# A decoder layer on one core: when an attention output projection is drawn as filler, and which queue fetches the last rows

## The chip, the cores and the metric

The kernel runs on one core of one Trainium2 chip. Its engines work in parallel, each through its own instructions in order: TensorE (PE in the profile, its weight loads PEld), VectorE (DVE), ScalarE (ACT), GpSimd (POOL) and SyncE (SP), which here only issues DMAs. DMAs issued by SP and ACT go through hardware queues, those issued by GpSimd through a software queue (q0 in the profile). The metric is the device time of one launch in microseconds, as the median of three runs, and it is to be small.

## The reference

Eight batches of 256 tokens with 512 features pass through one decoder layer in float32, with a plain layer norm (no weights) after each of three sublayers:

```
x = norm(x + attention(x))              # 16 heads of 32; Wq, Wk, Wv, then Wdown per head; softmax; Wup; Wo
r[t] = decay * r[t-1] + ctx[t]**2       # a running sum over the tokens of a batch, per feature
x = norm(x + x * r)                     # the "cross attention"
x = norm(x + silu(x @ gate.T) * (x @ up.T) @ down.T)   # 2048 wide; weights interpolated from control points
```

Wdown and Wup are folded into the projection weights by the kernel, so that a head is projected once.

## The kernel before, in words

The 2048 tokens are handled in four groups of 512 (`NG`), each of two batches. Attention runs as 32 steps, `steps[s] = (g, bb, quad)`: a step does four heads (`quad`) of one batch (`n = 2 * g + bb`). Steps 0 to 7 are the first group, 16 to 23 the third, 24 to 31 the last. I number them from 0, as the code does; batches too, so that the fifth batch is n = 4.

A step (lines 751 to 824) does this, each engine in the order of the program (`Ordered`, line 299):

- TensorE makes the scores of the *next* step (`scores(s + 1)`) in four PSUM buffers of the pool `ps_big`, then transposes the exponentials of this step, `es[0]` to `es[2]`, into buffers of `ps_mm` (tile `tr_e`). VectorE takes the maxima of the next scores (`nmax`), ScalarE their exponentials (`e`); the transposes are copied out (`eT`), the first and third by VectorE, the second and fourth by ScalarE.
- `fill(2)` draws two yields of filler, then the fourth transpose follows, then `fill(6)` (in the last group `fill(2)`).
- In odd steps the reciprocals of the softmax sums are spread and transposed (`tr_rec`, copied to `yT`). Then `weighted` multiplies the probabilities with the values into `av`. One `av` buffer serves two steps; it is read by VectorE (`yT = av * yT`) after the third transpose of the step after the odd one.

The pool `ps_mm` has four buffers. `tr_e`, `tr_rec`, `av`, the projections (`ps_q`, `ps_k`, `ps_v`), the output projection (`ps_o`), the transposes of the running sum (`tr_r`), and those of the feed-forward inputs (`tr_x`, `ps_mom`) all take their buffers from it.

Filler is a list of `units`, generators of which each `next` issues a piece for TensorE. A unit of four yields is one 128-row block of a projection of the next group (`project`, line 467, one matmul a yield, the eviction with the last), or one half of a batch's output projection (`output`, line 570). In the last group there are, in place of projections, `inputs(0)` and `inputs(1)` (line 700), eight yields each: four of transposes with their copies (`x2T`) and the DMAs to `xd`, and four of moment matmuls with copies (`mom`) and the DMAs to `md`. Before the scores of a new group, all units other than outputs are drawn to the end, in `fill(4)`.

Beside the units there are `chains`: `recur(n)` (line 485), which fetches the squared-to-be context `r` of a batch, squares it on GpSimd and runs four scans on VectorE, and `norms(n, qc, ...)` (line 589), which finishes 128 tokens after their output projection: the first norm (`nm`, a Square on ScalarE, `va` and `rs` on GpSimd, `x1`), the transposes of `r` (`tr_r`), then `h2`, `mx`, and the second norm. Every odd pass of a `fill` gives each chain one turn (`slot()`), and draws 0.62 of a weight chunk (`some_taps`). `recur` has its DMA in the first turn, the square in the third and the scans in the fifth to eighth; `norms` issues `tr_r` in its fourth turn and reads it in its fifth.

The tokens' rows for the residual come by `load_rows` (line 562) into the pool `rows`, of six buffers. At the first step of each batch n, the rows and the output projection of batch n - 1 are put up, and `recur(n)` is started. After step 31 the feed-forward part begins: `gate_up` (tiles `pg`, `pu`) for the first 512 tokens, then `fill(8)` with the output projection of batch 7, then the matmuls `y`.

Of the kernel before, what the change touches and what calls it, by code (L numbers as in the profile page):

```python
# [17 lines left out]
P = 128  # L18
B, T, D = 8, 256, 512
# [7 lines left out]
NG = NT // GT  # L27
# [288 lines left out]
def decoder_kernel(ctx: ExitStack, tc: tile.TileContext, x, xT, ctxT, wq, wkT, wvT, woT, wdownT, wup, decay, up_taps, down_taps, mom_f, sum_f, out, plan):  # L316
    nc = tc.nc
# [27 lines left out]
    nc = Ordered(tc)  # L345
    units, chains = [], []

    def slot():

        for c in list(chains):  # L350
            if next(c, c) is c:
                chains.remove(c)

    def fill(n):

        for i in range(n):
            if units:
                next(units[0][1])
                units[0][2] -= 1
                if not units[0][2]:  # L360
                    units.pop(0)
            if i % 2:
                slot()
                some_taps()
# [76 lines left out]
    def some_taps():  # L441
        made[0] += 0.62
        while made[0] >= 1:
            made[0] -= 1
            next(weights, None)
# [39 lines left out]
    def recur(n):  # L485

        r = last.tile([P, DC, T], F32, tag="r", name="r", bufs=2)
        nc.sync.dma_start(out=r, in_=ctxT[:, n * T : (n + 1) * T].rearrange("(c p) t -> p c t", p=P))
        rs[n] = r
        yield  # L490
        yield
        nc.gpsimd.tensor_tensor(r, r, r, ALU.mult)
        yield
        yield
        for ch in range(DC):
            nc.vector.tensor_tensor_scan(
                r[:, ch, :], dec[:, ch : ch + 1].to_broadcast([P, T]), r[:, ch, :], 0.0, ALU.mult, ALU.add
            )
            yield
# [61 lines left out]

    def load_rows(n):
        xs[n] = []
        for qc in range(2):
            x_t = rows.tile([P, D], F32, tag="row", name="x_t")
            r0 = (n * 2 + qc) * P
            nc.sync.dma_start(out=x_t, in_=x[r0 : r0 + P, :])
            xs[n].append(x_t)

    def output(n, qc):  # L570
# [112 lines left out]
    def windows(xd, xt, xg):  # L683


        past = SPAN * ND - D
        nc.sync.dma_start(out=xd[4 * (SPAN - past) + 3 :: 4, :], in_=xt[:past, 0, :])
        for h, odd, n, j0 in ((0, 0, NTILE // 2 - 1, 1), (1, NTILE - 1, NTILE // 2 - 1, 0)):
            for t, m, j in ((odd, 1, odd // 2), (2 * j0 + h, n, j0)):
                step = 4 * (lows[t + 2][0] - lows[t][0]) if m > 1 else 0  # L690
                from_ = bass.AP(xd.tensor, xd.offset + 4 * lows[t][0] * GT, [[GT, RAW], [step * GT, m], [1, GT]])
                nc.sync.dma_start(out=xg[h * K2 : h * K2 + RAW, j : j + m, :], in_=from_)
# [7 lines left out]
    def inputs(b):  # L700

        pool, mf = ffn["pool"], ffn["mf"]
        xt = pool.tile([P, DC, GT], F32, tag="x2T", name="x2T")
        xd = ffn["dram"].tile([4 * SPAN, GT], F32, tag="xd", name="xd")
        md = ffn["dram"].tile([1, 20 * NTILE, GT], F32, tag="md", name="md")
        xg = pool.tile([P, NTILE // 2, GT], F32, tag="xg", name="xg", bufs=2)
        xgs[b] = xg
        for c in range(DC):
            tr = ps_mm.tile([P, GT], F32, tag="mm", name="tr_x2")
            for t in range(TC):  # L710
                nc.tensor.transpose(tr[:, t * P : (t + 1) * P], x2[:, b * TC + t, c * P : (c + 1) * P], ident)
            (nc.vector.tensor_copy if c % 2 else nc.scalar.copy)(xt[:, c, :], tr)
            nc.gpsimd.dma_start(out=xd[c : 4 * (P - 1 - c) + c + 1 : 4, :], in_=xt[c:, c, :])
            if c:
                row = 4 * (SPAN - c) + c - 1
                nc.sync.dma_start(out=xd[row : row + 4 * c - 3 : 4, :], in_=xt[:c, c, :])
            yield
        if b > 1:
            reads.append(lambda: windows(xd, xt, xg))
        else:  # L720
            windows(xd, xt, xg)
        mo = ffn["mom"].tile([P, ND, GT], F32, tag="fin", name="mom")
        ps = {}
        for c in range(DC):
            for s in (c, c + 1):
                if s // 2 not in ps:
                    ps[s // 2] = ps_mm.tile([P, GT], F32, tag="mm", name="ps_mom")
                at = slice(s % 2 * K2, (s % 2 + 1) * K2)
                nc.tensor.matmul(
                    ps[s // 2][at, :],  # L730
                    lhsT=mf[:, c, s - c, :],
                    rhs=xt[:, c, :],
                    start=(s == c + 1 or c == 0),
                    stop=(s == c or c == DC - 1),
                )
            if c == 1:
                nc.vector.tensor_copy(mo[:, 0, :], ps[0])
            if c == DC - 1:
                nc.vector.tensor_copy(mo[:, 1, :], ps[1])
                nc.scalar.copy(mo[:K2, 2, :], ps[2][:K2, :])  # L740
                nc.gpsimd.dma_start(out=md[:, : 2 * P].rearrange("h (c p) t -> (h p) c t", p=P), in_=mo[:, :2, :])
                nc.gpsimd.dma_start(out=md[0, 2 * P :], in_=mo[:K2, 2, :])
                if b > 1:
                    reads.append(lambda: moments(md, xg))
                else:
                    moments(md, xg)
            yield
# [4 lines left out]
    for s, (g, bb, quad) in enumerate(steps):  # L752
        n = g * 2 + bb
        if quad == 0 and bb == 0:
            if g + 1 < NG:
                units += projections(g + 1, xT_g)
            else:
                first.close()
                open_inputs()
                units += [["i", inputs(0), 2 * DC], ["i", inputs(1), 2 * DC]]  # L760
        if quad == 0 and n:
            load_rows(n - 1)
            o = [["o", output(n - 1, qc), DC] for qc in range(2)]
            if bb and g + 1 < NG:
                units[1:1] = o[:1]
                units.append(o[1])
            else:
                units[1:1] = o
            chains.append(recur(n))
        more = s + 1 < len(steps)  # L770
        if more and steps[s + 1][0] != g:
            while any(u[0] != "o" for u in units):
                fill(4)
            if g + 2 < NG:
                xT_g = load_x(g + 2)
        if more:
            sc = scores(s + 1)
        after = []

        def ahead(j):  # L780
            if more:
                after.append(exponentials(s + 1, j, sc[j]))

        if quad % 2:
            rec = small.tile([P, 2, 8], F32, tag="rec", name="rec")
            nc.vector.reciprocal(rec, sums[n][:, :, quad // 2 * 8 : quad // 2 * 8 + 8])
            wide = att.tile([P, 2, 8, DH], F32, tag="wide", name="wide")
            nc.vector.tensor_copy(wide, rec.unsqueeze(3).to_broadcast([P, 2, 8, DH]))
        tr0 = transposed(es[0])
        ahead(0)  # L790
        eTs = [evicted(tr0, nc.vector.tensor_copy)]
        tr1 = transposed(es[1])
        tr2 = transposed(es[2])
        if pending is not None:
            y, av = pending
            nc.vector.tensor_tensor(y, av, y, ALU.mult)
            pending = None
        eTs.append(evicted(tr1, nc.scalar.copy))
        ahead(1)
        eTs.append(evicted(tr2, nc.vector.tensor_copy))  # L800
        fill(2)
        tr3 = transposed(es[3])
        ahead(2)
        eTs.append(evicted(tr3, nc.scalar.copy))
        ahead(3)
        fill(6 if g + 1 < NG else 2)
        if quad % 2:
            tr = ps_mm.tile([P, 2, T], F32, tag="mm", name="tr_rec")
            for q in range(2):
                for qc in range(2):  # L810
                    nc.tensor.transpose(
                        tr[:, q, qc * P : (qc + 1) * P],
                        wide[:, qc, q * 4 : q * 4 + 4, :].rearrange("p h r -> p (h r)"),
                        ident,
                    )
            y = last.tile([P, 2, T], F32, tag="yT", name="yT", bufs=4)
            nc.scalar.copy(y, tr)
            yTs.setdefault(n, []).append(y)
        else:
            av = ps_mm.tile([P, 2, T], F32, tag="mm", name="av")  # L820
        weighted(s, eTs, av)
        if quad % 2:
            pending = y, av
        es = after
# [202 lines left out]
```

## Time and profile before

| | us |
|---|---|
| median of three runs | 604.07 (603.5 to 604.6) |
| the profiled execution | 603.72 |
| its span, first to last instruction | 601.9 |
| TensorE busy | 577.3 (96%) |
| VectorE busy | 335.5 (56%) |
| ScalarE busy | 277.9 (46%) |
| GpSimd busy | 219.3 (36%) |

How to read it. The page gives busy time by engine, then the chain of work that ended last: from the last instruction back, at each step to what released it, or to the instruction before it on its engine. A line of a group reads "engine line operation out<-in, shape, count", then busy time and mean; in the timeline a line begins with its start and length in us, and ends in brackets with the idle time of the engine before it and what ended that. All instructions come from one helper (line 308), so tiles tell them apart. A matmul's end is modelled, so that a wait within a run of matmuls shows as a longer run. A 128x512 float32 matmul of the program stands as two MATMUL records in the trace.

### The profile page before, as it was taken

How to read it: one execution, taken by the hardware profiler on the slowest of the kernel's cores; microseconds unless marked ns; L12 is line 12 of the kernel's file. 1: busy time of each engine (PE TensorE's matmuls, PEld its weight loads, DVE VectorE, ACT ScalarE, POOL GpSimd, SP SyncE). 2: the span in 40 equal slices, each digit the busy share in tenths (PEclk: the TensorE clock that was granted, in tenths of full speed). 3: DMA queues.
4: the chain of work that ended last, by engine and by line, in shares of the span. 5: the costliest groups of instructions: out<-in, count | busy, mean ns of one | idle time of the engine just before them, and what ended most of it. 6: DMA issues, size and time to landing. Idle time of an engine off the chain costs nothing.

```text
span 601.9 us, 9688 instructions
## 1 busy us (share of the span) xinstructions
PE 577.3 (96%) x3346; PEld 292.0 (49%) x3346; DVE 335.5 (56%) x742; ACT 277.9 (46%) x820; POOL 219.3 (36%) x495
## 2 busy tenths in 40 slices
PE   9999999998899999999999999999999999999993
PEld 4544555555455555554554555444444434433432
DVE  0203634658676665886674777776926605714614
ACT  0114643655654554655455667665315404504502
POOL 0000997065544336444340311300272262142244
PEclk9999999999999999999999999999999999999998
DMA  8104253034224115323210564659328986984931
GB/s 294 64 0 157 80 167 114 27 98 144 74 71 141 36 54 175 105 71 96 79 36 2 158 152 102 173 152 216 65 72 223 205 233 179 227 213 134 212 142 70
DMA packets 38961, 75.50 MB, mean 125 GB/s; under 512 B 3937, under 2 KB 8289, under 8 KB 38913
## 3 DMA queue, kind: packets, MB, share of 16 engines
q1 hardware_dynamic: 34576, 62.75, 39.4%
q0 software_dynamic: 3328, 10.96, 5.5%
q10 hardware_dynamic: 1008, 1.18, 0.7%
q8 instruction: 26, 0.43, 0.3%
q14 instruction: 23, 0.18, 0.1%
HBM read 42.86 MB, written 11.04 MB: 90 GB/s over the span
## 4 chain that ended last, share of the span: by engine, by line
PE 82%; DVE 10%; ACT 3%; DMA 2%; issue 2%; POOL 1%; POOLq 0%; DVEq 0%; SPq 0%; ACTq 0%
PE y L308 12%; PE ps_k L308 9%; PE ps_v L308 9%; PE ps_o L308 8%; PE ps_q L308 6%; PE tr_e L308 6%; PE sc L308 5%; PE pg L308 5%; PE ps_s L308 5%; PE av L308 5%; PE pu L308 5%; DVE nmax L308 3%; PE ps_mom L308 2%; ACT e L308 2%; DVE eT L308 2%
## 5 line engine op out<-in xcount | busy, mean ns | idle before, releaser
L308 ACT ACTIVATE e<-sc,nmax 128x256 f32<-128x256 f32 x256 | 120.2, 480 | 102.1 <-DVE nmax L308 102.1
L308 DVE TENSOR_REDUCE nmax<-sc 128x2 f32<-128x512 f32 x128 | 84.5, 682 | 73.6 <-PE sc L308 67.7
L308 POOL TENSOR_TENSOR taps<-taps 128x256 f32<-128x256 f32 (+1 forms) x144 | 89.0, 618 | 33.1 <-DMA taps<-in_down_taps 26.3
L308 PEld LDWEIGHTS tr_e<-ident,e 128*128 128x128 f32 x512 | 56.9, 140 | 25.2 <-issue 22.5
L308 PE MATMUL tr_e<-ident,e 128*128 128x128 f32 x512 | 68.3, 276 | 0.5 <-DVE eT L308 0.4
L308 PE MATMUL y<-inter,wd 32*128 32x512 f32 x512 | 63.0, 598 | 0.0
L308 PE MATMUL ps_o<-w_o,yT 128*128 128x512 f32 x128 | 60.0, 600 | 2.6 <-DVE eT L308 2.3
L308 PE MATMUL ps_k<-xT_g,w_k 128*128 128x512 f32 x128 | 58.8, 601 | 0.6 <-DVE eT L308 0.6
L308 PE MATMUL ps_v<-w_v,xT_g 128*128 128x512 f32 x128 | 58.6, 598 | 0.4 <-DVE eT L308 0.4
L308 PE MATMUL ps_q<-xT_g,w_q 128*128 128x512 f32 x128 | 58.2, 596 | 0.0
L308 POOL TENSOR_SCALAR va<-ss 128x1 f32<-128x1 f32 x32 | 7.3, 227 | 136.8 <-ACT x L308 86.6
L308 POOL TENSOR_TENSOR rs<-va,neghalf 128x1 f32<-128x1 f32 x48 | 28.9, 602 | 69.4 <-DVE va L308 66.7
L308 ACT ACTIVATION_READ_ACCUMULATOR e<-sc,nmax 128x1 f32 x256 | 53.2, 208 | 0.0
L308 DVE TENSOR_TENSOR inter<-pu,sg 128x512 f32<-128x512 f32 x64 | 41.2, 686 | 18.3 <-PE pu L308 9.4
L308 ACT ACTIVATE sg<-pg 128x512 f32<-128x512 f32 x64 | 37.2, 596 | 18.4 <-PE pg L308 18.4
L308 DVE COPY eT<-tr_e 128x512 f32<-128x512 f32 x64 | 43.8, 684 | 0.5 <-PE tr_e L308 0.4
L308 PEld LDWEIGHTS y<-inter,wd 32*128 32x128 f32 x512 | 26.7, 184 | 32.7 <-issue 27.0
L308 PE MATMUL av<-eT,v_g 128*32 128x256 f32 x512 | 36.7, 385 | 5.0 <-ACT eT L308 2.7
L308 ACT COPY eT<-tr_e 128x512 f32<-128x512 f32 x64 | 37.5, 585 | 2.4 <-PE tr_e L308 2.4
L308 POOL TENSOR_TENSOR r<-r 128x1024 f32<-128x1024 f32 x8 | 15.2, 1895 | 63.6 <-DMA r<-in_ctxT 63.6
L308 PE MATMUL sc<-k_g,q_g 32*128 32x256 f32 x512 | 37.4, 401 | 0.2 <-ACT e L308 0.2
L308 PEld LDWEIGHTS ps_o<-w_o,yT 128*128 128x128 f32 x128 | 22.8, 190 | 26.4 <-issue 21.5
(98 smaller groups left out, 737.5 us busy)
## 6 DMA issues: line engine op xcount, KB each, us to landing
nat<-inter SPq DMA_DIRECT2D x64, 256.0 KB
taps<-in_down_taps SPq DMA_DIRECT2D x40, 256.0 KB
taps<-in_up_taps SPq DMA_DIRECT2D x16, 384.0 KB
xg<-xd SPq DMA_DIRECT2D x8, 616.0 KB
r<-in_ctxT SPq DMA_DIRECT2D x8, 512.0 KB
x_t<-in_x SPq DMA_DIRECT2D x16, 256.0 KB
fin<-sum POOLq DMA_DIRECT2D x16, 256.0 KB, 5.1
out<-h SPq DMA_DIRECT2D x16, 256.0 KB
```

The lines of the kernel that those rows point to most:

```text
L308: return lambda *a, **k: self.tc.keep_in_program_order(f(*a, **k))
```

## The change

- Projection and output yields drawn after the fourth transpose: 6 in the first two groups as before, 5 in the third, 3 in the last (2 before).
- In the third group, at its second batch, both halves of the output projection of batch 4 are put at the end of the units; before, the first half stood second and the other at the end.
- In the last group, at its first batch, the output projection of batch 5 is put ahead of the last unit, and the rows of batch 5 and `recur(6)` come two steps later (at quad 2). At its second batch the rows of batch 6 are put up with the output projection as before, and `recur(7)` comes two steps later.
- Rows of batches 5, 6 and 7, and the context of batches 6 and 7, are fetched by GpSimd's queue in place of SP's.

```diff
     def recur(n):
 
         r = last.tile([P, DC, T], F32, tag="r", name="r", bufs=2)
-        nc.sync.dma_start(out=r, in_=ctxT[:, n * T : (n + 1) * T].rearrange("(c p) t -> p c t", p=P))
+        (nc.sync if n + 2 < 2 * NG else nc.gpsimd).dma_start(out=r, in_=ctxT[:, n * T : (n + 1) * T].rearrange("(c p) t -> p c t", p=P))
...
     def load_rows(n):
         xs[n] = []
+        queue = nc.sync if n + 3 < 2 * NG else nc.gpsimd
         for qc in range(2):
             x_t = rows.tile([P, D], F32, tag="row", name="x_t")
             r0 = (n * 2 + qc) * P
-            nc.sync.dma_start(out=x_t, in_=x[r0 : r0 + P, :])
+            queue.dma_start(out=x_t, in_=x[r0 : r0 + P, :])
...
                 units += [["i", inputs(0), 2 * DC], ["i", inputs(1), 2 * DC]]
+        if n and quad == (0 if g + 1 < NG else 2):
+            if g + 1 < NG or not bb:
+                load_rows(n - 1)
+            chains.append(recur(n))
         if quad == 0 and n:
-            load_rows(n - 1)
             o = [["o", output(n - 1, qc), DC] for qc in range(2)]
-            if bb and g + 1 < NG:
+            if bb and g + 2 == NG:
+                units += o
+            elif bb and g + 2 < NG:
                 units[1:1] = o[:1]
                 units.append(o[1])
+            elif g + 1 == NG and not bb:
+                units[-1:-1] = o
             else:
+                if g + 1 == NG:
+                    load_rows(n - 1)
                 units[1:1] = o
-            chains.append(recur(n))
...
-        fill(6 if g + 1 < NG else 2)
+        fill((6, 6, 5, 3)[g])
```

## The prediction

> **What bounds the kernel now.** I read the page first: which engine is busy, and which ends the chain of waits.
>
> ```profile
> span 601.9 us, 9688 instructions
> PE 577.3 (96%) x3346; PEld 292.0 (49%) x3346; DVE 335.5 (56%) x742; ACT 277.9 (46%) x820; POOL 219.3 (36%) x495
> PE 82%; DVE 10%; ACT 3%; DMA 2%; issue 2%; POOL 1%; POOLq 0%; DVEq 0%; SPq 0%; ACTq 0%
> ```
>
> TensorE carries 82% of the chain. The change neither adds nor removes a matmul, so only TensorE's waits can move the time. The sums by window (span, length, then busy time of PE, PEld, DVE, ACT, POOL) show where they are: the third group of tokens (steps 16 to 23, and the end of step 15), the last group (24 to 31), the head of the feed-forward part.
>
> ```profile
> 230.88:323.60 92.72, 92.16 (x545) 49.80 (x545) 62.62 (x144) 51.74 (x172) 39.88 (x74) 1.00 0.28 88
> 331.62:402.40 70.78, 64.56 (x496) 37.09 (x493) 54.62 (x128) 45.98 (x154) 15.83 (x25) 1.00 0.56 146
> 402.40:424.28 21.88, 21.88 (x93) 9.85 (x89) 15.33 (x34) 12.78 (x24) 1.49 (x4) 1.00 0.98 214
> ```
>
> Only the last group has room: 6.2 us of visible idle time, and matmuls stretched by waits inside them. The waits of TensorE in that window name the causes: evictions (x2T, mom, eT) that come late.
>
> ```profile
> PE av L308 <- DVE x2T L308: 2.3, 2, 1.2
> PE av L308 <- ACT eT L308: 1.3, 2, 1.0
> PE tr_rec L308 <- DVE mom L308: 0.8, 1, 0.8
> PE ps_mom L308 <- DVE mom L308: 0.8, 1, 0.8
> ```
>
> The resource behind it is the pool ps_mm, four PSUM buffers for everything but scores. One is always av (kept from an even step until the yT multiply of the next even step). The three transposes that open a step take the others. Step 7 has no filler, so its fourth transpose asks for a fifth buffer and waits for the first eT, which DVE ended at 139.97. TensorE's order of time there:
>
> ```profile
> 138.10 1.53 PE L308 MATMUL tr_e<-ident,e 128*128 128x128 f32 x12
> 140.03 0.66 PE L308 MATMUL tr_e<-ident,e 128*128 128x128 f32 x4 [0.39 <-DVE eT L308]
> ```
>
> Step 29 shows what a fuller pool costs: with av, a moment sum and tr_r held, the fourth transpose waits for a moment copy, and the last moment matmul for the eviction after it.
>
> ```profile
> 374.66 1.15 PE L308 MATMUL sc<-k_g,q_g 32*128 32x256 f32 x16
> 375.74 1.53 PE L308 MATMUL tr_e<-ident,e 128*128 128x128 f32 x12
> 377.20 1.98 PE L308 MATMUL ps_mom<-x2T,mf 128*64 128x512 f32 x8
> 379.11 0.66 PE L308 MATMUL tr_r<-ident,r 128*128 128x128 f32 x4
> 379.92 0.66 PE L308 MATMUL tr_e<-ident,e 128*128 128x128 f32 x4 [0.15 <-DVE mx L308]
> 380.51 1.94 PE L308 MATMUL ps_mom<-x2T,mf 128*64 128x512 f32 x6
> 383.23 1.07 PE L308 MATMUL ps_mom<-x2T,mf 128*64 128x512 f32 x2 [0.78 <-DVE mom L308]
> ```
>
> **The change, part by part.** A unit of filler is four yields; one yield of projection is two 128x512 matmuls, 0.86 us. Before, a step draws 2 and then 6 (last group: 2), so every unit ends inside its step. After, the third group draws 2+5 and the last 2+3: units straddle steps and hold a buffer across the opening transposes.
>
> What is moved, by counting yields: the third group has 64 (48 of projections, 8 each of batches 3 and 4). Steps 16 to 22 serve 49; at step 23 the loop that empties projections serves 8 ahead of the scores, and 2+5 the remaining 7. So the matmuls of batch 4 (the fifth) still end in step 23; their norms go to the last group. There 32 yields are served 5 a step, so that step 30 gets 2 and step 31 none.
>
> Third group. The third transpose normally starts 0.97 us after the first (two of three in 1.46): 376.71 in step 29. With a unit held it waits for the first eT, as the moment matmul at 377.20 did: +0.49. With tr_r held too, the second waits to 377.20, ends at 377.69, ACT's eT takes to 378.4, and the third starts at 378.45: +1.74. Units are held into steps 17, 18, 21, 22 and 23. Into step 19 both are, since with three slots a step the fourth slot of norms (x1, tr_r) of batch 3's second half falls last in step 18, and h2, which frees the buffer, in the next. 5 x 0.49 + 1.74 = 4.2. Two waits of 0.44 at steps 17 and 19 lie at the same place; I take +3.8. TensorE is 92.16 of 92.72 busy, so nothing covers this and a gain over 0.6 is excluded. Bounds 0 (the buffer handed out happens to be free) to +4.6.
>
> Last group, step by step, each time from the start of its scores, by these rows: DVE pitch 0.6 (nmax, eT, copy, h1, h2, mx, scan), ACT 0.91 for a pair of e, 0.47 to 0.58 for a copy, 0.8 for a Square. Now 8.54, 9.34, 8.61, 8.02, 8.53, 11.16, 9.25, 7.33 (start to start of scores; the last ends at 402.40).
> Step 24: four transposes of x2 as now, plus one moment yield in the wait ahead of av: 8.8.
> Step 25: av, the moment buffer and tr_r are held. Transposes at 1.08, 2.54, 3.8; the second moment yield needs the buffer of the third eT, 5.15; two moment yields to 6.9, tr3 to 7.4, the fourth to 8.35. DVE meanwhile does copy, h2, mx ahead of the third nmax, so that e ends at 8.8, eT at 9.4 and the copy of the moment sums at 9.15; two output yields and tr_r run from there to 11.35, tr_rec waits for ACT's copy, 11.9, av 12.9.
> Step 26: a unit and tr_r held. The unit ends within the first fill (5.35), and DVE's h1, h2, mx stand ahead of nmax: nmax 8.2, e 9.2, eT 9.8, the last 5/8 of av 0.65: 10.5.
> Step 27: h1 and a norm ahead of nmax, tr_r and three tr_x share the free buffers; the third x2T comes from ACT at 9.0, then tr_rec and av: 10.6.
> Step 28: norm, scan, h2 and mx ahead of nmax: 8.9, e 9.9, eT 10.45; av ends at 12.0.
> Step 29: 8.77 of work and 1.74 for two held: 10.5.
> Step 30: two yields; h1, a norm and two Squares ahead: eT 8.45: 9.15.
> Step 31: 7.33 less four yields (3.43) plus 0.9 of bare eviction: 4.8.
> The sum is 79.25 for 70.78: +8.5. Lower bound: step 7 without filler took 7.92 (137.03 to 144.95); if steps 24 to 29 kept their lengths, with 8.88 where 5 yields fill one (+1.1), step 30 fell to 7.9 and step 31 to 4.9, it would be -2.6. Between these ends I take the upper: step 29's row shows the wait itself.
>
> GpSimd's queue. Six row loads (128 pieces of 2 KB) and two of r (512 pieces of 1 KB) move from SP to POOL. The nearest issue on POOL is xd, of 128 pieces:
>
> ```profile
> L308 POOL DMA_DIRECT2D xd<-x2T x16: 530/552/775, 337.2 to 502.2; - x16
> DMA to landing us min/median/max: 2.3/3.5/4.8
> ```
>
> 6 x 0.55; md with 256 pieces took 0.75 to 0.82, so I estimate 1.3 for r: 5.9 us of POOL, which is busy 15.8 of 70.8. What is queued behind is va and rs of the norms. SP loses eight issues of about 0.4, with nobody waiting: h never waited for x_t. I cost the loads at nothing; the cover is that x_t of batch 5, issued about when step 26 starts behind md, lands by 2 to 4 and h1 comes at 5.45. If it lands as late as md did at worst (9.3), h1 and all behind it on DVE come 3.5 us later: that is the upper end of the last group, +12.
> The Trainium skill ("DMA: Bandwidth & Descriptors", Specifications) speaks against this part: first byte after about 1 us by GpSimd, 0.6 by the sync path. If all eight loads were on the path, that would be 3.2 us more; by the rows none is.
>
> Moved later: scans of batch 7 (four of 0.68 on DVE) go into the head of the feed-forward part, where DVE is busy 15.3 of 21.9, hidden under matmuls. Moved earlier from there: two groups of tr_r, 0.44 each on TensorE: -0.9 (bounds -0.9 and 0). Taps: 92 slots are needed, reached in step 22 before and in step 23 after; the weights are read at 402, so nothing.
>
> Sum: 601.9 + 3.8 + 8.5 - 0.9 = 613.3 of span; the profiled execution took 603.72, 1.8 more than its span, so 615.1. The median of the runs is 604.07, 0.35 above it. I say 615.
>
> The longest idle time of TensorE is now 2.00 us (at 160.58), at a granted clock of 1.00. Step 30 may idle 2.9.
> "TensorE: Matmul & The Clock Gate" (What's actually happening) lets the clock fall to half after an idle window of about 3.4 us; one such fall would add some 1.7 us as an estimate. No row here shows it.
>
> **The rivals.**
> Faster: the even draw does what a balance should. For it: 6.2 us idle in the last group, and steps 30 and 31 get shorter. Against it: steps 7 and 29. Price -2.6 - 0.9, third group free: 600.2. It decides if the third transpose starts under 1.1 us after the first in steps 25, 26 and 29.
> Half: the third group pays, and in the last the fifth yield covers as much as the held buffers cost: 603.7 + 3.8 - 0.9 = 606.6. For it: six waits there are for ACT or DVE, which more filler hides.
> Late rows: the software queue lands x_t of batch 5 late; 618.6. Against it: four transfers of xd on that queue landed in 2.3 to 4.8.
> Nothing: the order of the matmuls is nearly kept, as the count of yields shows; if buffers never bind, 603.7.
>
> **How the numbers follow.** My forecast 0.58 (own range 610 to 618), late rows 0.06, half 0.19, faster 0.13, nothing 0.04. A measurement of this kernel tells 0.2%, 1.2 us, from no change. Faster 0.13, same 0.04, slower 0.83. The range is 605 to 620: it leaves out faster and nothing, 0.17, and a little of the tails.
>
> **What would show it.** Right: the third group grows from 92.7 to about 96.5, with waits of about 0.5 of the third tr_e for DVE's eT in steps 17, 18, 21 to 23, 1.7 in step 19; the last group grows from 70.8 to about 79, step 25 above 12, step 31 under 5.5; the head falls to about 21. Wrong: opening transposes without waits, or h waiting for x_t, or a last group under 71.

## The result, and the profile after

The changed kernel takes 622.1 us (median of 4 runs, 618.98 to 622.89) against 603.79 for the kernel before beside it: a ratio of 1.0305, 95% interval 1.0289 to 1.0321. It is slower by 18.3 us. The forecast was slower, 615, with a range to 620; the time lies above the range.

The page of the changed kernel, in the lines shown of before (span, busy time, the granted clock in 40 slices, the chain of waits):

```profile
span 620.4 us, 9686 instructions
...
PE 583.9 (94%) x3346; PEld 296.7 (48%) x3346; DVE 337.1 (54%) x742; ACT 279.0 (45%) x820; POOL 223.0 (36%) x503
...
PEclk9999999999999999999999999789999999999998
...
PE 83%; DVE 9%; ACT 3%; issue 2%; DMA 1%; POOL 0%; POOLq 0%; DVEq 0%; ACTq 0%
```

The same line of the clock before:

```profile
PEclk9999999999999999999999999999999999999998
```

The count of matmuls is the same, yet TensorE is busy 6.6 us longer, and the clock shows a dip to 0.7 that the kernel before does not have. The sums by window (span, length, busy time of PE, PEld, DVE, ACT, POOL, then the granted clock) take the third group together with step 23, then the last group, then the feed-forward part:

```profile
230.33:333.63 103.30, 100.00 (x602) 53.89 (x601) 63.53 (x137) 57.22 (x190) 38.34 (x71) 1.00 0.25 79
333.63:420.25 86.62, 71.58 (x509) 40.15 (x505) 60.58 (x147) 47.95 (x157) 22.97 (x38) 0.94 0.45 117
420.25:620.40 200.15, 187.93 (x1084) 85.01 (x1080) 96.11 (x218) 69.43 (x132) 66.02 (x212) 0.99 0.69 170
```

Before, the same stretches took 100.74 (92.72 and the 8.02 of step 23), 70.78 and 199.50; the first and the last of them:

```profile
230.88:331.62 100.74, 100.17 (x605) 54.56 (x604) 67.16 (x153) 57.55 (x192) 39.88 (x74) 1.00 0.26 81
402.40:601.90 199.50, 188.46 (x1092) 82.84 (x1088) 96.15 (x222) 69.99 (x134) 67.50 (x214) 0.99 0.69 169
```

So the third group lost 2.56, the last 15.84, the feed-forward part 0.65, and the first two groups ended 0.55 earlier: 18.5 of span.

**The opening transposes wait.** TensorE's order at the start of step 17, where an unfinished output projection holds a buffer, and of step 19, where a projection and `tr_r` do:

```profile
250.09 1.09 PE L308 MATMUL tr_e<-ident,e 128*128 128x128 f32 x8
251.53 0.66 PE L308 MATMUL tr_e<-ident,e 128*128 128x128 f32 x4 [0.35 <-DVE eT L308]
252.02 1.45 PE L308 MATMUL ps_o<-w_o,yT 128*128 128x512 f32 x3
...
272.51 0.66 PE L308 MATMUL tr_e<-ident,e 128*128 128x128 f32 x4
273.95 0.66 PE L308 MATMUL tr_e<-ident,e 128*128 128x128 f32 x4 [0.79 <-DVE eT L308]
275.34 0.66 PE L308 MATMUL tr_e<-ident,e 128*128 128x128 f32 x4 [0.73 <-ACT eT L308]
275.83 1.88 PE L308 MATMUL ps_q<-xT_g,w_q 128*128 128x512 f32 x4
```

From the first transpose to what follows the third, 1.44 to 1.46 us is normal. In step 17 it is 1.93, in step 19 3.32: 0.49 and 1.88 more. (The idle time in brackets is less than that, since the ends of matmuls are modelled.) Over the last group the waits of TensorE are now:

```profile
PE tr_e L308 <- DVE eT L308: 3.5, 6, 0.8
PE av L308 <- ACT eT L308: 3.4, 2, 2.6
PE ps_o L308 <- DVE mom L308: 1.9, 1, 1.9
...
PE tr_e L308 <- ACT eT L308: 1.5, 2, 0.7
```

**The clock falls.** The same order for steps 28 to 30 (the scores at 390.96 open step 29, those at 404.07 open step 30):

```profile
385.47 0.66 PE L308 MATMUL tr_r<-ident,r 128*128 128x128 f32 x4 [0.17 <-DVE h L308]
388.04 1.12 PE L308 MATMUL ps_o<-w_o,yT 128*128 128x512 f32 x2 [1.92 <-DVE mom L308]
389.10 1.94 PE L308 MATMUL av<-eT,v_g 128*32 128x256 f32 x16
390.96 1.90 PE L308 MATMUL sc<-k_g,q_g 32*128 32x256 f32 x16
...
396.26 3.43 PE L308 MATMUL ps_o<-w_o,yT 128*128 128x512 f32 x4
...
409.33 0.63 PE L308 MATMUL av<-eT,v_g 128*32 128x256 f32 x6
412.60 1.53 PE L308 MATMUL av<-eT,v_g 128*32 128x256 f32 x10 [2.64 <-ACT eT L308]
```

Scores that take 1.15 elsewhere take 1.90, and four output matmuls 3.43 in place of 1.88. The sums by window, cut where the clock changes, give a granted clock of 0.50 in stretches of 3.41 us, each after a stretch in which TensorE had much idle time:

```profile
385.72:389.13 3.41, 1.50 (x10) 0.50 (x10) 3.34 (x11) 2.31 (x10) 0.79 (x1) 1.00 0.74 152
389.13:392.54 3.41, 3.41 (x33) 1.79 (x32) 1.11 (x5) 0.57 (x3) 0.56 (x1) 0.50 0.94 207
...
409.61:413.02 3.41, 0.77 (x14) 0.27 (x9) 2.48 (x10) 2.64 (x10) 1.02 (x3) 1.00 0.00 0
413.02:416.44 3.42, 3.42 (x18) 2.55 (x13) 2.50 (x3) 1.46 (x5) 2.92 (x4) 0.50 0.00 0
```

A third such stretch runs from 395.96 to 399.37.

### The profile page after: what moved, and what is told of

Its sections match the earlier page's. It is cut to its first block, busy times and chain, and to the rows that moved or that the text cites. A ratio compares the mean times of both kernels' runs of the same rounds, so it can differ in the third digit from the quotient of the medians.

```text
span 620.4 us, 9686 instructions
## 1 busy us (share of the span) xinstructions
PE 583.9 (94%) x3346; PEld 296.7 (48%) x3346; DVE 337.1 (54%) x742; ACT 279.0 (45%) x820; POOL 223.0 (36%) x503
## 4 chain that ended last, share of the span: by engine, by line
PE 83%; DVE 9%; ACT 3%; issue 2%; DMA 1%; POOL 0%; POOLq 0%; DVEq 0%; ACTq 0%
PE y L308 11%; PE ps_k L308 9%; PE ps_v L308 9%; PE ps_o L308 9%; PE ps_q L308 8%; PE tr_e L308 7%; PE sc L308 5%; PE av L308 5%; PE pg L308 5%; PE ps_s L308 5%; PE pu L308 4%; DVE nmax L308 3%; PE ps_mom L308 2%; DVE eT L308 2%; ACT e L308 2%
## 5 line engine op out<-in xcount | busy, mean ns | idle before, releaser
L308 PE MATMUL tr_e<-ident,e 128*128 128x128 f32 x512 | 73.1, 282 | 8.6 <-DVE eT L308 6.4
L308 DVE TENSOR_TENSOR inter<-pu,sg 128x512 f32<-128x512 f32 x64 | 41.2, 686 | 18.6 <-PE pu L308 10.5
```

The costliest lines, as they stand in the source:

```text
L308: return lambda *a, **k: self.tc.keep_in_program_order(f(*a, **k))
```

## The experiments

Three theories were set against each other. **Held buffers**: draws of 7 and 5 yields cut units of four, which keep one of the four ps_mm buffers over the opening transposes. **Queue**: the loads by GpSimd come late or hold up GpSimd. **Late norms and sums**: work on VectorE that was put off by two steps or a group.

### Draws back, and draws alone

```diff
-        fill((6, 6, 5, 3)[g])
+        fill(6 if g + 1 < NG else 2)        # in the changed kernel; the reverse in the kernel before
```

> The changed kernel with the old draws (6 in three groups, 2 in the last), all else as changed. Held buffers: no unit straddles a step, so the opening transposes wait no more, the clock does not fall, and 18 us come back: 602 to 606. Queue (the loads by GpSimd are late): nothing of it is undone, above 612. Late norms and sums (work on VectorE put off by two steps): rows and sums are still put off, above 610.

> The kernel before with the new draws alone (6, 6, 5, 3). Held buffers: 616 to 624, with the opening transposes of steps 17 to 19, 21 to 23 waiting 0.5 to 1.9 us and those of the last group too. Queue: 602 to 606. Late norms and sums: 604 to 608.

With the old draws the changed kernel takes 605.75 (ratio to before 1.0038, 1.0024 to 1.0053): 16.4 of the 18.3 us come back. With the new draws alone the kernel before takes 617.59 (1.0228, 1.0203 to 1.0253). The draws carry the loss both ways. The rest of the change costs about 2.4 us by itself, and with the draws some 4.5. In the profile of the draws alone, steps 17, 18 and 19 take 10.99, 11.43 and 12.38, as in the changed kernel, and the clock falls twice in the last group.

### The third group alone, the last group alone

```diff
-        fill((6, 6, 5, 3)[g])
+        fill((6, 6, 5, 2)[g])               # or (6, 6, 6, 3)
```

> The changed kernel with 5 in the third group and 2 in the last. Held buffers: the third group keeps its 2.5 us over the kernel before (steps 17 to 19, 21 to 23), the last stays at about 72.8 us as with the old draws: 607 to 609. If the third group's draws upset the last group by where the norms of batch 4 fall: above 612.

> The changed kernel with 6 in the third group and 3 in the last. Held buffers: the third group as before, the last group still 83 to 88 us: 617 to 621. If the harm came from the third group: 606 to 609.

610.81 (1.0129, 1.0102 to 1.0155) and 614.83 (1.0191, 1.0172 to 1.0211). Against the 605.75 with both draws back, the third group's draw costs about 5 us and the last group's about 9; together they would make 620, the changed kernel has 622.1. The second ran 2 us under what was expected, the first 2 over. In the profile of the first, the third group with step 23 takes 103.28 us, 2.5 over the kernel before, as expected. That execution took 609.16 and another 609.47, at a mean clock of 0.996; the other two took 612.15 and 612.22, at 0.993. So part of the 5 us is probably the clock, though no profile of the slower two shows it.

### Whole units with the same delay

Fewer yields a step do two things: units straddle, and work is put off to step 23. This kernel puts off as much (8 yields a step, but 4 in steps 19 and 22) without cutting a unit; in the last group it has the old draws.

```diff
-        fill((6, 6, 5, 3)[g])
+        fill(2 if g + 1 == NG else 2 if s in (19, 22) else 6)
```

> The changed kernel with the old draws in the last group and, in the third, 8 yields a step but 4 in steps 19 and 22: as much work is put off to step 23 as with 7 a step, the norms of batch 4 fall as late, but no unit straddles a step. Held buffers: the third group loses nothing, 603 to 607. Work put off: as with 7 a step, 608 to 611.

605.67 (1.0042, 1.0028 to 1.0056), the same as with the draws back. The sums by window for the third group with step 23, of this kernel and then of the one with 7 yields a step:

```profile
230.06:330.67 100.61, 99.78 (x601) 54.18 (x601) 63.01 (x138) 56.97 (x190) 39.19 (x73) 1.00 0.26 81
```
```profile
229.68:332.96 103.28, 99.99 (x601) 53.90 (x600) 63.34 (x137) 57.16 (x190) 38.12 (x71) 1.00 0.24 80
```

TensorE is busy for the same time; the 2.7 us between them are idle time at the opening transposes. In the third group, putting the work off costs nothing: it is the cut units. The last group of this kernel:

```profile
330.67:403.46 72.79, 66.20 (x501) 37.69 (x497) 56.32 (x140) 46.58 (x155) 21.01 (x34) 1.00 0.52 139
```

Of the 15.84 us that the last group lost, 2.0 are thus there with the old draws too. Such a test with whole units was not made in the last group: five yields a step always cut units of four.

### The clock

The idle time of TensorE in steps 28 and 30 is filled with matmuls that nobody reads.

```diff
             if c == DC - 1:
+                for _ in range(2 if b == 1 else 0):
+                    nc.tensor.matmul(ps[2][K2:, :], lhsT=mf[:, c, 0, :], rhs=xt[:, c, :], start=True, stop=True)
...
             av = ps_mm.tile([P, 2, T], F32, tag="mm", name="av")
+            for _ in range(3 if s == 30 else 0):
+                nc.tensor.matmul(av, lhsT=w_o[:, 0, :P], rhs=w_o[:, 0, :], start=True, stop=True)
```

> The changed kernel with idle TensorE time filled: two spare matmuls (1.7 us) ahead of the copies in the last moment yield of inputs(1), into rows of the buffer that nobody reads, and three (2.6 us) into the av buffer of step 30 before its real matmuls, which overwrite them. The output stays the reference's. Clock: two of the three stretches of half clock (389 to 392 and 413 to 416) go, and in spite of 4.3 us more work the time falls by 2 to 6 us, to 616 to 620. If the clock does not hang on idle time: the stretches stay and the time rises by up to 4 us.

617.56 (1.0254, 1.0225 to 1.0283): with five matmuls more it is 4.5 us faster than the changed kernel. In the profiled execution no stretch of half clock is left ahead of the end. The last group by window, and TensorE's order in steps 28 and 30:

```profile
333.71:415.87 82.16, 71.26 (x518) 39.04 (x515) 60.05 (x146) 47.87 (x157) 23.03 (x38) 1.00 0.46 123
```
```profile
383.91 3.17 PE L308 MATMUL ps_mom<-x2T,mf 128*64 128x512 f32 x10
387.01 0.65 PE L308 MATMUL tr_r<-ident,r 128*128 128x128 f32 x4
388.11 1.13 PE L308 MATMUL ps_o<-w_o,yT 128*128 128x512 f32 x2 [0.44 <-DVE mom L308]
389.17 1.07 PE L308 MATMUL av<-eT,v_g 128*32 128x256 f32 x16
...
406.03 2.74 PE L308 MATMUL av<-w_o 128*128 128x512 f32 x6
408.70 1.74 PE L308 MATMUL av<-eT,v_g 128*32 128x256 f32 x16
```

The spare work stands where TensorE waited, the following steps start as early or earlier, and `av` at 389.17 takes 1.07 where it took 1.94. The last group falls from 86.62 to 82.16. So some 4.5 of its 15.84 us are the clock, which the waits pull down, and 11.4 are lost at full clock.

### The queue

```diff
-        (nc.sync if n + 2 < 2 * NG else nc.gpsimd).dma_start(out=r, ...
+        nc.sync.dma_start(out=r, ...                # and the rows likewise; the reverse in the kernel before
```

> The changed kernel with every load on SP's queue again. Held buffers: 620 to 624, nothing of it touches the buffers. Queue: 604 to 610.

> The kernel before with the rows of batches 5 to 7 and the context of batches 6 and 7 on GpSimd's queue, nothing else. Held buffers: 603 to 605. Queue: 610 and more. A small loss of up to 3 us would be GpSimd's time for the issues, ahead of va and rs.

Both theories missed here; the small loss allowed for in the kernel before came, but from a wait for the buffer of `r` and not from GpSimd's time to issue. With all loads on SP the changed kernel takes 631.32 (1.0461, 1.0433 to 1.0489), 9 us more than with GpSimd; with the loads on GpSimd the kernel before takes 606.73 (1.0054, 1.0039 to 1.0069), 3.4 more. The order decides each time. On SP, the late row loads of batch 5 stand behind `xg<-md`, which waits for the moments to land in DRAM; they are issued at 361.65, and in step 26, which takes 19.95 in place of 10.91, VectorE waits for them. From the waits and from TensorE's order of that kernel:

```profile
DVE h L308 <- DMA x_t<-in_x: 9.2, 1, 9.2
```
```profile
370.44 1.07 PE L308 MATMUL av<-eT,v_g 128*32 128x256 f32 x6 [5.96 <-DVE h L308]
```

On GpSimd, in the kernel before, the context of batch 7 is due two steps earlier, when its buffer is still read by `tr_r` of batch 5. The queue is in order, so `xd`, `va` and `rs` stand behind it:

```profile
379.13 0.78 POOL L308 DMA_DIRECT2D r<-in_ctxT  x1 [7.30 <-PE tr_r L308]
379.89 1.09 POOL L308 DMA_DIRECT2D xd<-x2T  x2
381.06 0.18 POOL L308 TENSOR_SCALAR va<-ss 128x1 f32<-128x1 f32 x1
381.32 0.56 POOL L308 TENSOR_TENSOR rs<-va,neghalf 128x1 f32<-128x1 f32 x1
```

VectorE waits 2.4 us for that `rs`, the copy of the moments behind it holds TensorE for 2.81 (step 29 takes 14.55 in place of 11.16), and the clock falls once. The late start of the rows and of `recur` and the change of queue belong together; each without the other loses.

### What holds up the last group before the change

In the last group of the kernel before, norms and scans stand on VectorE ahead of the third `nmax`; the third head's `e` waits for it on ScalarE, the fourth `eT` for `e`, and `av` for `eT`. Two edits go at that: give the chains no turn in the first draw and two in the second, or copy the fourth transpose ahead of the exponentials.

```diff
-        fill(2)
+        fill(2, 1 if g + 1 < NG else 0)     # second argument: turns of the chains
...
-        fill(6 if g + 1 < NG else 2)
+        fill(*((6, 1) if g + 1 < NG else (2, 2)))
```

> The kernel before; in the last group the chains take no turn in the first draw and two in the second, so no norm or scan stands on VectorE ahead of the third and fourth nmax. If the waits of the last group before the change are those of VectorE's order, 3 to 6 us go: 598 to 601. If they are buffers alone: 602 to 606.

609.45 (1.011, 1.0093 to 1.0126): slower, which neither side expected. Steps 24 and 26 do get shorter (8.54 to 8.08, 8.61 to 7.65), so VectorE's order was a cause. But a norm that has its fourth turn last in a step now keeps `tr_r` over the opening transposes, the same fault as in the changed kernel. Of step 29, where the wait is longer than a held buffer alone makes it, since VectorE is late there too (it waited 1.80 us for `rs`, and its first `nmax` came at 379.12):

```profile
380.46 0.66 PE L308 MATMUL tr_e<-ident,e 128*128 128x128 f32 x4 [2.56 <-DVE eT L308]
```

The other edit touches no buffer:

```diff
-        ahead(2)
         eTs.append(evicted(tr3, nc.scalar.copy))
+        ahead(2)
         ahead(3)                            # in the last group; in a second kernel in all steps
```

> The kernel before; in the last group ScalarE copies the fourth transpose out ahead of the third head's exponentials, so that av no longer waits for nmax and e. If the waits of av in steps 24, 26, 28, 30 are this order (0.7 to 1.4 us each), 2 to 4 us go: 599 to 602. If buffers set the pace: 603 to 605.

> The same swap in the changed kernel. The long waits of av for ScalarE (in steps 26 and 30, 1.4 and some 3.4 us) go, and with the one of step 30 the last stretch of half clock: 614 to 618. Held buffers remain, so it does not come under 612.

> The kernel before with the swap of e9 in all 32 steps. Step 7 has no filler and its av waits 1.4 us for ScalarE's eT, as those of the last group did; the other steps hold enough filler behind the fourth transpose. If that is so, 1 us more goes than with the swap in the last group alone: 597 to 600. If the later exponentials hold up the next scores in full steps: 600 to 604.

In the kernel before it gives 599.28 (0.994, 0.9923 to 0.9958): 3.9 us faster than the kernel before, and 23 faster than the changed one. Steps 24, 26 and 28 take 6.99, 7.65 and 7.49, from 8.54, 8.61 and 8.53. In step 26 `av` ran in two pieces with a wait for `eT` between them (356.14 and 357.12); now it is one. The two lines of before, then the one of this kernel:

```profile
356.14 0.63 PE L308 MATMUL av<-eT,v_g 128*32 128x256 f32 x6
357.12 1.05 PE L308 MATMUL av<-eT,v_g 128*32 128x256 f32 x10 [0.35 <-ACT eT L308]
```
```profile
353.40 1.07 PE L308 MATMUL av<-eT,v_g 128*32 128x256 f32 x16
```

In all steps it gives 598.56 (0.9926, 0.9897 to 0.9954), which is not told apart from 599.28. In the changed kernel it gives 615.91 (1.021, 1.0187 to 1.0233): one stretch of half clock is still there, and the held buffers.

## Why the prediction was right or wrong

**The sign and the mechanism of the waits were right.** Four ps_mm buffers, units that straddle, waits at the opening transposes, and the count of yields that leaves batch 4's matmuls in step 23: the draws carry the loss (both ways), and the kernel with whole units has none of it in the third group. For the last group the evidence is weaker. The draws cause its loss, but only 5.0 of some 15 us of TensorE's waits there are at the transposes `tr_e`; the others are for other copies and for norms that come late on VectorE and ScalarE, and how much of those goes back to held buffers is not shown.

**Third group, +3.8: measured +2.56.** The waits themselves came as worked out: 0.49, 0.50, 1.88, 0.49, 0.54 and 0.49 in steps 17, 18, 19, 21, 22 and 23, in sum 4.4 against 4.2. What I set off was too little: both old waits of 0.44 went, not half of them, and one `tr_r` of batch 4 (0.44) left the group, which I had only counted where it arrived. That makes 3.1. Of the remaining 0.5, most is likely that fewer units open behind the first three transposes: four matmuls take 1.98 us where they open a unit there and 1.88 where they go on with one. The sign as I wrote it, 92.7 growing to 96.5, did not show: without step 23 the stretch took 92.31, and the growth is in step 23, which took 10.99 for 8.02.

**Last group, +8.5: measured +15.84.** This term failed. The steps, worked out and measured: 8.8 and 8.83, 12.9 and 13.44, 10.5 and 10.91, 10.6 and 10.65, 12.0 and 13.5, 10.5 and 13.11, and for steps 30 and 31 together 13.95 and 16.17. Up to step 27 the working holds within 0.6. From step 28 on it took every matmul at full clock. With the waits filled, at full clock, the steps are 8.83, 13.44, 10.9, 10.66, 12.63, 10.7 and 15.0: 82.16 against my 79.25. So of the 7.3 us that were missing, 4.5 are the clock and 2.9 rows set a little short, most in steps 25, 28, 30 and 31. Step 31, which was to come under 5.5, took 6.2 (5.5 with the waits filled). The step that failed is the sentence on the clock. I saw a wait of 2.9 us coming in step 30 and weighed it against a rule of the Trainium skill of an idle window of about 3.4 us ("TensorE: Matmul & The Clock Gate", What's actually happening), so that one fall at most was thought of, worth 1.7, and the sum left it out. The runs showed three falls, the first after 1.91 us of idle time within a stretch of 3.41; the rule was too lax for this kernel, and the measurement decides. The range failed for the same reason: its upper end came from late rows, not from the clock. The kernel with the waits filled took 617.56, inside the range.

**GpSimd's queue at nothing: right for this change, for a narrower reason than I gave.** `h` did not wait for `x_t` in the changed kernel (they landed 3.3 to 6.2 us after issue; with the old draws it waited 0.92 for one), the two waits of VectorE for `rs`, 1.06 and 1.04, come behind `xd` and the square of `recur` and not behind a load, and the issue of `r`, which I set at 1.3, took 0.76 to 0.80. But the same loads cost 3.4 us in the order of before, and SP in their place costs 9: the late row loads need GpSimd. I had written that nobody waits on SP for them, which was a row of the old order.

**Head of the feed-forward part, -0.9: measured 0.** The two `tr_r` left, and the matmuls `y` start 0.75 earlier after the first `pg` (21.13 against 21.88). The scans of batch 7, which I called hidden, are not: the first `tr_r` of batch 7 waits for the last of them.

```profile
443.50 0.33 PE L308 MATMUL tr_r<-ident,r 128*128 128x128 f32 x1 [0.50 <-DVE r L308]
```

By the next `tr_x`, 48.17 us after `pg`, the two kernels are level (48.19 before). The 0.65 us by which the whole part is longer arise later, and I can't assign them. This term was 0.9 too hopeful and the third group's 1.2 too dark; that the two nearly cancel is luck.

**The rivals.** Faster fell: the third transpose starts 2.84 us after the first in step 25 (343.53 to 346.37), some 2.0 in step 26 and 2.83 in step 29 (392.79 to 395.62), beyond the 1.1 that was to decide. Half and nothing fell with the draws. Late rows did not happen here, but with SP it did, at 9 us and not 3.5.

## What to carry to other kernels

When filler is drawn by count, draw whole units, or count which buffers a half unit and its epilogue keep over the next burst of allocations: here one held buffer of four cost 0.5 us a step, two cost 1.9. Where an engine waits often, price the waits twice, once as time and once by what they do to TensorE's clock. And a load moved to another queue is judged by what stands ahead of it and behind it there, so a queue and the time of issue have to be chosen together.

## What the runs showed of the hardware that was not expected

The clock falls without a long pause. Where a profile has several falls inside the kernel, they lie whole multiples of 3.41 us apart (389.13, 395.96 and 413.02 in the changed kernel). Cutting the profiles of this case into stretches of 3.41 on that grid and adding the idle time of TensorE in each gives the following (rough figures, since matmul ends are modelled). Ten of the eleven falls from full clock inside a kernel follow a stretch with 1.86 us of idle time or more (1.86, 1.91, 1.99, 2.06, 2.08, 2.43, 2.58, 2.64, 3.2, 3.41, in six kernels). Stretches at full clock that have up to 1.85 are not followed by a fall, with one exception: 395.96 follows a stretch with 1.52, which itself came right after a stretch of half clock. In the other direction one stretch does not fit either: in the kernel with the copy first in all steps, 1.93 us idle from 157.20 to 160.61 brought no fall. So a little over half a stretch idle, in one piece or several, mostly goes with a fall, and the share alone does not settle it.

The same program falls in one execution and not in another: the changed kernel took 618.98 at a mean clock of 0.992 and 622.0 to 622.9 at 0.987, and the one with filled waits 617.0 to 617.6 at 0.995 to 0.996, and 620.37 at 0.990. That would follow if the grid does not start with the kernel, which I infer and no run here tests. That the idle share of a stretch matters, I infer from these profiles; that idle time is the cause is shown by the filled waits, after which the profiled execution had no fall left.
